# First three batch tiles run group by group, first loads in one line, W turns spread, x turned first

## Chip, cores, metric

One core of one Trainium2 chip. The metric is the device time of one execution in microseconds (us). Ratios are the mean time of one kernel's fast runs over that of the other's fast runs of the same rounds, so they are not quite the ratio of the medians that are quoted beside them.

## The reference

For 4096 rows of 32 vectors of 64 numbers, every pair i < j (496 pairs) has its own 64 x 64 matrix:

```python
idx_i, idx_j = np.triu_indices(F, k=1)          # F = 32, 496 pairs
vi, vj = inputs[:, idx_i, :], inputs[:, idx_j, :]
vidots = jnp.einsum('bpd,pde->bpe', vi, W)
return vidots * vj                              # (4096, 496, 64) float32
```

The output is 520 MB, the inputs 33.6 MB and 8.1 MB.

## The kernel before

A *tile* is 128 batch rows; there are 32, two to an x *block*. Each tile goes through 46 *steps*; a step multiplies x_i with the matrices of up to 16 pairs on PE into PSUM, and then multiplies the result with x_j into an output buffer, on VectorE (DVE), or for some steps by a copy on ScalarE (ACT) and a product on GpSimd (POOL). Five *groups* of steps fill five output buffers' worth, each sent out by one DMA.

W (496 rows of 64 x 64) is loaded in four pieces. Each piece is used only after four *orders* (an SBUF-to-SBUF copy that reorders it) and four *turns* (eight transposes on PE and a copy out of PSUM). x is turned likewise.

```python
groups = [(0, 3), (3, 7), (7, 11), (11, 17), (17, F - 1)]   # 90, 106, 90, 105, 105 pairs
aside = (1, 3, 5, 7, 9, 11, 13)                              # ACT + POOL instead of DVE
xpool = tile_pool(bufs=2); tpool = tile_pool(bufs=3); opool = tile_pool(bufs=3)
...
def load_w(c):
    pool, tag = ((opool, "ot"), (xpool, "xs"), (const, "w3"), (xpool, "xs"))[c]
    ...
    nc.sync.dma_start(out=raw[c][: b - a, :], in_=wflat[a:b])
...
for c, at in enumerate([None, (2, 4, 5, 7), (9, 11, 13, 15), (20, 22, 25, 28)]):
    ...                                   # order and turn k of piece c before step at[k]
new_x(0)
load_x(0, nc.scalar, 0, 1)
load_w(0); load_w(1); load_x(0, nc.sync, 1, NB); load_w(2)
...
for s in range(NBLK * NB * NS):           # tile by tile
    ...
            else:
                c, k = args
                turn_w(c, k, order_w(c, k, (v, p)[k % 2]), a)   # v: DVE, p: POOL, a: ACT
                if k == NU - 1 and c == 1: load_w(3)
                if k == NU - 1 and c == 3: new_x(1); load_x(1, nc.scalar)
    ...
    if pa + m == end:
        nc.sync.dma_start(out=..., in_=ot[:, : end - base, :])
```

Here W pieces 1 and 3 borrow the second x buffer, so x block 1 is loaded last.

## Time and profile before

| | us |
|---|---|
| median of 4 runs | 1359.68 (1359.32 to 1359.97) |
| span of the profiled run | 1357.5 |
| DMA busy from 60 to 1330 us | 99 to 100% |
| bytes | 562.92 MB |

The lines that carry this are in the prediction. Read them with one rule: where DMA is always busy, a microsecond of DMA idle anywhere is a microsecond at the end. In the lines, PEld is PE's weight load, SP is SyncE; SPq and ACTq lines are DMAs being issued on the queue of SP or ACT; `raw` is a loaded piece of W, `rp` an ordered one, `ptw` and `ptx` are turns of W and x in PSUM, `ps` holds products, `ot` is an output buffer, `xs` an x block. Two stretches of the kernel before that the prediction doesn't show, for the comparison below (stretch, its length, busy us of PE, PEld, DVE, ACT and POOL with counts, PE clock, DMA share, GB/s):

```profile
80.00:90.00 10.00, 10.00 (x66) 5.87 (x66) 7.81 (x10) 5.06 (x5) 7.64 (x4) 1.00 1.01 433
90.00:100.00 10.00, 9.20 (x64) 5.57 (x62) 7.19 (x10) 3.04 (x3) 4.78 (x3) 1.00 1.00 428
```

### The profile page before, as it was taken

The page shows a single profiled execution, that of the slowest core. Times are in us where ns is not written, and L with a number is a line of the kernel's source. Part 1 is how long each engine was busy: PE and PEld are TensorE (multiplying, and loading weights), DVE is VectorE, ACT ScalarE, POOL GpSimd, SP SyncE. Part 2 cuts the span into 40 slices and gives each one's busy share as a digit, 9 for nine tenths or more (in the row PEclk, how much of TensorE's full clock was granted, in tenths as well). Part 3 has the DMA queues.
Part 4 walks back from the last instruction along what each step waited for, and adds up shares of the span by engine and source line. Part 5 has one row for each costly group of instructions (what it writes and reads, how often), then busy time and mean ns, then how long its engine had stood idle before and what let it go on. Part 6 is the DMA issues. An engine that isn't in the chain of part 4 may idle for free.

```text
span 1357.5 us, 17867 instructions
## 1 busy us (share of the span) xinstructions
PE 1171.5 (86%) x7424; PEld 681.2 (50%) x7424; DVE 951.3 (70%) x1259; ACT 371.1 (27%) x367; POOL 546.2 (40%) x253
## 2 busy tenths in 40 slices
PE   5998988888888888988889888899888889888894
PEld 4554554545455454554545445455454545545552
DVE  5686876767677676766667767677776777767783
ACT  3432322222222222222322222222222322223220
POOL 4544433443333443334434334433344433444441
PEclk9998998989999999998989999999898999999997
DMA  7999999999999999999999999999999999999997
GB/s 291 388 430 431 426 424 431 431 422 426 401 424 413 430 423 412 428 409 431 410 417 425 413 433 407 421 423 410 428 412 424 426 409 424 406 431 428 417 419 335
DMA packets 26128, 562.92 MB, mean 415 GB/s; under 512 B 2896, under 2 KB 2896, under 8 KB 2896
## 3 DMA queue, kind: packets, MB, share of 16 engines
q1 hardware_dynamic: 23744, 529.28, 92.0%
q10 hardware_dynamic: 2304, 32.51, 5.7%
q8 instruction: 58, 0.95, 0.3%
q14 instruction: 22, 0.18, 0.0%
HBM read 41.68 MB, written 520.09 MB: 414 GB/s over the span
## 4 chain that ended last, share of the span: by engine, by line
DMA 50%; PE 23%; DVE 18%; POOL 4%; issue 3%; ACT 0%; DVEq 0%; SPq 0%; POOLq 0%; ACTq 0%
DMA out_dram<-ot 49%; PE ps L192 19%; DVE ot L209 18%; PE ptx L113 4%; POOL ot L207 3%; DMA raw<-in_L_rec_W_dram 1%; POOL rp L94 1%; PE ptw L103 0%; ACT tmp L206 0%; DVE rp L94 0%; DVEq L209 0%; DVE xT L117 0%; ACT wT L106 0%; SPq L211 0%; POOLq L207 0%
## 5 line engine op out<-in xcount | busy, mean ns | idle before, releaser
L209 DVE TENSOR_TENSOR ot<-ps,xs 128x1024 f32<-128x1024 f32 (+15 forms) x1248 | 938.6, 807 | 378.4 <-DMA out_dram<-ot 195.3
L192 PE MATMUL ps<-wT,xT 64*128 64x512 f32 (+14 forms) x6272 | 1025.2, 467 | 118.0 <-DVE ot L209 105.5
L192 PEld LDWEIGHTS ps<-wT,xT 64*128 64x128 f32 x6272 | 554.0, 193 | 554.6 <-DVE ot L209 281.9
L207 POOL TENSOR_TENSOR ot<-tmp,xs 128x1024 f32<-128x1024 f32 x224 | 527.3, 2360 | 623.5 <-ACT tmp L206 397.7
L206 ACT COPY tmp<-ps 128x1024 f32<-128x1024 f32 x224 | 226.7, 1012 | 465.5 <-PE ps L192 460.6
L117 ACT COPY xT<-ptx 128x1024 f32<-128x1024 f32 x127 | 128.5, 1012 | 470.2 <-PE ptx L113 470.2
L113 PE MATMUL ptx<-ident,xs 128*128 128x128 f32 x1024 | 143.8, 285 | 48.9 <-DVE ot L209 34.3
L113 PEld LDWEIGHTS ptx<-ident,xs 128*128 128x128 f32 x1024 | 113.2, 144 | 95.4 <-issue 51.3
L71 POOL MEMSET xs<- 128x64 f32 x16 | 2.4, 151 | 146.7 <-DVE ot L209 146.7
L94 POOL COPY rp<-raw 128x1024 f32<-128x1024 f32 (+1 forms) x7 | 16.1, 2299 | 16.1 <-DMA raw<-in_L_rec_W_dram 11.8
L106 ACT COPY wT<-ptw 128x1024 f32<-128x1024 f32 (+1 forms) x15 | 14.7, 984 | 28.1 <-PE ptw L103 28.1
L103 PE MATMUL ptw<-ident,rp 128*128 128x128 f32 (+1 forms) x128 | 17.0, 280 | 3.2 <-DVE rp L94 2.0
L94 DVE COPY rp<-raw 128x1024 f32<-128x1024 f32 (+1 forms) x9 | 11.0, 1233 | 12.3 <-DMA raw<-in_L_rec_W_dram 11.9
L103 PEld LDWEIGHTS ptw<-ident,rp 128*128 128x128 f32 (+1 forms) x128 | 14.1, 145 | 10.2 <-issue 5.6
L106 ACT ACT_TABLE_LOAD x1 | 1.3, 1283 | 1.2 <-PEq L229 1.2
L117 DVE COPY xT<-ptx 128x1024 f32<-128x1024 f32 x1 | 1.2, 1208 | 0.0
L106 DVE COPY wT<-ptw 128x1024 f32<-128x1024 f32 x1 | 1.2, 1208 | 0.0
masks.py:197 POOL MEMSET ident<- 128x128 f32 x1 | 0.2, 205 | 0.3 <-POOLq L229 0.3
masks.py:199 POOL TENSOR_SCALAR_AFFINE_SELECT ident<-ident 128x128 f32<-128x128 f32 x1 | 0.3, 292 | 0.0
L229 POOL MEMSET const-float32-0.0<- 128x1 f32 x1 | 0.1, 98 | 0.2 <-issue 0.2
L229 POOL MEMSET const-bfloat16-1.0<- 128x1 bf16 x1 | 0.1, 101 | 0.0
L229 POOL MEMSET const-uint8-127<- 128x1 uint8 x1 | 0.1, 101 | 0.0
(1 smaller groups left out, 0.1 us busy)
## 6 DMA issues: line engine op xcount, KB each, us to landing
out_dram<-ot SPq DMA_DIRECT2D x64, 3360.0 KB, 16.2
out_dram<-ot SPq DMA_DIRECT2D x64, 2880.0 KB, 16.7
out_dram<-ot SPq DMA_DIRECT2D x32, 3392.0 KB, 17.2
xs<-in_r_inputs_dram ACTq DMA_DIRECT2D x15, 2048.0 KB, 16.6
raw<-in_L_rec_W_dram SPq DMA_DIRECT2D x3, 2048.0 KB, 15.6
raw<-in_L_rec_W_dram SPq DMA_DIRECT2D x1, 1792.0 KB, 15.7
xs<-in_r_inputs_dram ACTq DMA_DIRECT2D x1, 1024.0 KB, 11.4
xs<-in_r_inputs_dram SPq DMA_DIRECT2D x1, 1024.0 KB, 17.7
```

Of the source, the lines that this page charges most:

```text
L71: nc.gpsimd.memset(xs[blk][:, 0, :], 0.0)
L94: copy(rp[:r], src[:, k * EU : (k + 1) * EU])
L103: nc.tensor.transpose(pt[:, n, :r], rp[:r, n].rearrange("p h d -> p (h d)"), ident[:r, :r])
L106: copy(wT[c][:, :, k * EU : (k + 1) * EU], pt[:, :, :r].rearrange("p e r -> p r e"))
L113: nc.tensor.transpose(pt[:, n, :], xs[blk][:, s : s + 2, :].rearrange("p f d -> p (f d)"), ident)
L117: copy(xT, pt)
L192: nc.tensor.matmul(ps[:, h, lo - pa : hi - pa, :], xT[blk, kt, n // RUN][h * D : (h + 1) * D, n % RUN, :], wT[c][h * D : (h + 1) * D, lo - ...
L206: nc.scalar.copy(tmp, src)
L207: nc.gpsimd.tensor_mul(dst, tmp, xj)
L209: nc.vector.tensor_mul(dst, src, xj)
L229: nc = _bacc.Bacc("TRN2", target_bir_lowering=False, num_devices=1)
```

## The change

Intent: fill the DMA gap at the start. x is loaded and turned first; all first loads stand in one queue, x block 1 among them; the first three tiles run group by group, so that a piece of W serves three tiles before the next is needed; the first output is cut so that 61 pairs leave early. Because x block 1 now sits in the second x buffer from the start, W piece 3 gets the buffer of piece 2 and is loaded when piece 2 has been ordered.

```diff
-    groups = [(0, 3), (3, 7), (7, 11), (11, 17), (17, F - 1)]
+    bounds = [0, p0[3], p0[6] + CH, p0[11], p0[17], NP]      # 90, 97, 99, 105, 105 pairs
-    tpool = ... bufs=3
+    tpool = ... bufs=4
-        pool, tag = ((opool, "ot"), (xpool, "xs"), (const, "w3"), (xpool, "xs"))[c]
+        pool, tag = ((opool, "ot"), (opool, "ot"), (const, "w3"), (const, "w3"))[c]
+    LEAD = 3
+    sched = [
+        (t, s) for g in range(len(groups)) for t in range(LEAD) for s in range(NS) if steps[s][0] == g
+    ]
+    sched += [(t, s) for t in range(LEAD, NT) for s in range(NS)]
+    for c, orders, turns in (
+        (1, (2, 4, 8, 10), (4, 7, 12, 15)),
+        (2, (17, 22, 27, 32), (19, 24, 29, 34)),
+        (3, (43, 44, 45, 46), (48, 50, 52, 54)),
+    ):
+    no_aside = range(41, 55)
 ...
-    load_x(0, nc.scalar, 0, 1)
+    load_x(0, nc.sync, 0, 1)
     load_w(0)
     load_w(1)
     load_x(0, nc.sync, 1, NB)
     load_w(2)
+    new_x(1)
+    load_x(1, nc.sync)
 ...
+    xT[0, 0, 0] = turn_x(0, 0, 0, a)
+    for k, copy in enumerate((v, v, v, a)):
+        rps[0, k] = order_w(0, k, copy)
+    for k, copy in ((0, a), (3, a), (1, v), (2, a)):
+        turn_w(0, k, rps.pop((0, k)), copy)
 ...
+                rps[c, k] = order_w(c, k, p if c > 1 and k % 2 else v)
+                if (c, k) == (2, NU - 1):
+                    load_w(3, nc.scalar)
 ...
-        if i in aside and c0 == 0:
+        if i in aside and c0 == 0 and s not in no_aside:
+        ends = (p0[2], end) if s < NS and (t, g) == (0, 0) else (end,)
+        if pa + m in ends:                    # first output: 61 and 29 pairs
```

More of the change, by code (lines that the diff above doesn't have):

```diff
@@ L42 @@
     p0 = [i * (F - 1) - i * (i - 1) // 2 for i in range(F)]
-    groups = [(0, 3), (3, 7), (7, 11), (11, 17), (17, F - 1)]
-    cap = max(p0[b] - p0[a] for a, b in groups)
+    bounds = [0, p0[3], p0[6] + CH, p0[11], p0[17], NP]
+    groups = list(zip(bounds[:-1], bounds[1:]))
+    cap = max(b - a for a, b in groups)
     aside = (1, 3, 5, 7, 9, 11, 13)
@@ L55 @@
     xtpool = ctx.enter_context(tc.tile_pool(name="xtpool", bufs=4))
-    tpool = ctx.enter_context(tc.tile_pool(name="tpool", bufs=3))
+    tpool = ctx.enter_context(tc.tile_pool(name="tpool", bufs=4))
     opool = ctx.enter_context(tc.tile_pool(name="opool", bufs=3))
@@ L81, with load_w @@
     NU = E2 // EU
-    def load_w(c: int):
+    def load_w(c: int, eng=nc.sync):
         a, b = wrows[c]
-        pool, tag = ((opool, "ot"), (xpool, "xs"), (const, "w3"), (xpool, "xs"))[c]
+        pool, tag = ((opool, "ot"), (opool, "ot"), (const, "w3"), (const, "w3"))[c]
         raw[c] = pool.tile([P, D * D], F32, tag=tag, name=f"raw_{c}")
-        nc.sync.dma_start(out=raw[c][: b - a, :], in_=wflat[a:b])
+        eng.dma_start(out=raw[c][: b - a, :], in_=wflat[a:b])
     def order_w(c: int, k: int, copy):
@@ L122 @@
         (g, i, c0, min(CH, F - 1 - i - c0))
+        for i in range(F - 1)
+        for c0 in range(0, F - 1 - i, CH)
         for g, (a, b) in enumerate(groups)
-        for i in range(a, b)
-        for c0 in range(0, F - 1 - i, CH)
+        if a <= p0[i] + c0 < b
     ]
@@ L130 @@
         first.setdefault(i, s)
+    LEAD = 3
+    NT = NBLK * NB
+    sched = [
+        (t, s) for g in range(len(groups)) for t in range(LEAD) for s in range(NS) if steps[s][0] == g
+    ]
+    sched += [(t, s) for t in range(LEAD, NT) for s in range(NS)]
+    place = {ts: n for n, ts in enumerate(sched)}
     AHEAD = 4
     due: dict = {}
-    for t in range(NBLK * NB):
+    for t in range(NT):
         for q in range(F // RUN):
-            at = t * NS + (first[q * RUN - 1] if q else 0) - AHEAD
+            at = place[t, first[q * RUN - 1] if q else 0] - AHEAD
             due.setdefault(max(0, at), []).append(("x", t // NB, t % NB, q))
-    for c, at in enumerate([None, (2, 4, 5, 7), (9, 11, 13, 15), (20, 22, 25, 28)]):
-        for k in range(NU) if c else ():
-            due.setdefault(at[k], []).append(("w", c, k))
+    for c, orders, turns in (
[3 rows of a table added]
+    ):
+        for k in range(NU):
+            due.setdefault(orders[k], []).append(("order", c, k))
+            due.setdefault(turns[k], []).append(("turn", c, k))
+    no_aside = range(41, 55)
     LATE = 6
+    loads = {place[blk * NB, LATE]: blk + 1 for blk in range(2, NBLK - 1)}
+    loads[place[LEAD, LATE]] = 2
     new_x(0)
-    load_x(0, nc.scalar, 0, 1)
+    load_x(0, nc.sync, 0, 1)
     load_w(0)
@@ L149 @@
     load_w(2)
+    new_x(1)
+    load_x(1, nc.sync)
     v, p, a = nc.vector.tensor_copy, nc.gpsimd.tensor_copy, nc.scalar.copy
-    xT = {(0, 0, 0): turn_x(0, 0, 0, v)}
+    xT, rps = {}, {}
+    xT[0, 0, 0] = turn_x(0, 0, 0, a)
     due[0] = [d for d in due[0] if d != ("x", 0, 0, 0)]
-    rps = [order_w(0, k, copy) for k, copy in ((0, v), (1, p))]
-    turn_w(0, 0, rps[0], a)
-    rps.append(order_w(0, 2, v))
-    turn_w(0, 1, rps[1], a)
-    rps.append(order_w(0, 3, v))
-    turn_w(0, 2, rps[2], v)
-    turn_w(0, 3, rps[3], a)
-    ot = None
-    for s in range(NBLK * NB * NS):
-        t, st = divmod(s, NS)
+    for k, copy in enumerate((v, v, v, a)):
+        rps[0, k] = order_w(0, k, copy)
+    for k, copy in ((0, a), (3, a), (1, v), (2, a)):
+        turn_w(0, k, rps.pop((0, k)), copy)
+    ots = {}
+    for s, (t, st) in enumerate(sched):
         blk, kt = divmod(t, NB)
         g, i, c0, m = steps[st]
-        if st == LATE and kt == 0 and blk and blk + 1 < NBLK:
-            new_x(blk + 1)
-            load_x(blk + 1, nc.scalar)
+        if s in loads:
+            new_x(loads[s])
+            load_x(loads[s], nc.scalar)
         for what, *args in due.get(s, ()):
@@ L172 @@
                 xT[tuple(args)] = turn_x(*args, a)
+            elif what == "turn":
+                turn_w(*args, rps.pop(tuple(args)), a)
             else:
                 c, k = args
-                turn_w(c, k, order_w(c, k, (v, p)[k % 2]), a)
-                if k == NU - 1 and c == 1:
-                    load_w(3)
-                if k == NU - 1 and c == 3:
-                    new_x(1)
-                    load_x(1, nc.scalar)
-        base, end = p0[groups[g][0]], p0[groups[g][1]]
+                rps[c, k] = order_w(c, k, p if c > 1 and k % 2 else v)
+                if (c, k) == (2, NU - 1):
+                    load_w(3, nc.scalar)
+        base, end = groups[g]
         pa = p0[i] + c0
         if pa == base:
-            ot = opool.tile([P, cap, D], F32, tag="ot", name=f"ot_{t}_{g}")
+            ots[t] = opool.tile([P, cap, D], F32, tag="ot", name=f"ot_{t}_{g}")
+        ot = ots[t]
         ps = psum.tile([P, 2, CH, E2], F32, tag="ps", name=f"ps_{s}")
@@ L209 @@
             nc.vector.tensor_mul(dst, src, xj)
-        if pa + m == end:
+        ends = (p0[2], end) if s < NS and (t, g) == (0, 0) else (end,)
+        if pa + m in ends:
+            n0 = p0[2] if len(ends) > 1 and pa + m == end else base
             nc.sync.dma_start(
-                out=rows_of(out, blk).rearrange("(p k) n d -> p k n d", k=NB)[:, kt, base:end, :],
-                in_=ot[:, : end - base, :],
+                out=rows_of(out, blk).rearrange("(p k) n d -> p k n d", k=NB)[:, kt, n0 : pa + m, :],
+                in_=ot[:, n0 - base : pa + m - base, :],
             )
```

## The prediction

> **What bounds the kernel now.** I read the page's slices first, then ten-microsecond windows of the start, then the order of time.
>
> ```profile
> DMA  7999999999999999999999999999999999999997
> GB/s 291 388 430 431 426 424 431 431 422 426 401 424 413 430 423 412 428 409 431 410 417 425 413 433 407 421 423 410 428 412 424 426 409 424 406 431 428 417 419 335
> HBM read 41.68 MB, written 520.09 MB: 414 GB/s over the span
> ```
>
> Each slice is 34 us. After the first, the DMA engines are busy nine tenths or more and move 400 to 431 GB/s. 562.92 MB at 427 GB/s alone would take 1318 us of 1357.5. So the kernel is bound by the writing of its output, and compute only has to keep that fed. Only the first two slices fall clearly short. The end is no worse: the last output is issued at 1342.1 with about one earlier output still queued.
>
> The windows of the start (columns: stretch, its length, busy us of PE, PEld, DVE, ACT and POOL with counts, PE clock, DMA share, GB/s):
>
> ```profile
> 0.00:10.00 10.00, 0.00 (x0) 0.00 (x0) 0.00 (x0) 1.28 (x1) 0.79 (x7) 1.00 0.85 322
> 10.00:20.00 10.00, 6.10 (x40) 5.66 (x40) 7.91 (x6) 2.94 (x3) 3.83 (x2) 1.00 0.99 424
> 20.00:30.00 10.00, 9.97 (x56) 5.34 (x57) 6.71 (x7) 4.29 (x5) 5.92 (x3) 1.00 0.22 95
> 30.00:40.00 10.00, 10.00 (x69) 6.30 (x69) 6.64 (x7) 5.75 (x7) 6.79 (x4) 1.00 0.97 365
> 40.00:50.00 10.00, 8.34 (x60) 5.37 (x61) 5.46 (x8) 4.93 (x5) 7.87 (x4) 1.00 1.00 363
> 50.00:60.00 10.00, 9.09 (x66) 5.57 (x64) 4.99 (x8) 5.75 (x6) 8.13 (x5) 1.00 1.01 414
> ```
>
> By 60 us 19.83 MB have moved, 46.4 us of work at 427: 13.6 us are lost. 2.5 of these belong to the first ten (nothing moves at once; the change keeps that). **About 11 us can be won at most**: 7.8 in 20 to 30, where the first loads are over and no output is ready, and 3 in 30 to 50, where the last piece of W is read at about 290 GB/s between two outputs. From 60 to 160 us I find no loss.
>
> In that gap PE is the busy engine. In order of time:
>
> ```profile
> 20.03 1.94 PE L192 MATMUL ps<-wT,xT 64*128 64x512 f32 x8 [1.10 <-ACT wT L106]
> ...
> 21.90 1.09 PE L103 MATMUL ptw<-ident,rp 128*128 128x128 f32 x8
> ...
> 22.92 1.88 PE L192 MATMUL ps<-wT,xT 64*128 64x512 f32 x8
> ...
> 29.97 0.35 SPq L211 DMA_DIRECT2D out_dram<-ot  x1
> 30.41 0.38 SPq L88 DMA_DIRECT2D raw<-in_L_rec_W_dram  x1
> ```
>
> From the starts: 31 pairs take 1.87 us (0.0605 us a pair), a turn of eight blocks 1.02 us. Check: the first group is 90 pairs with three W turns, 5.45 + 3.06 = 8.5, so PE should end at 28.5; it ended near 28.6. The second (106 pairs, five turns) should end at 40.1; near 40.4. The output is issued 1.1 to 1.4 us after PE's end. I use this chain below. One pair is 32.8 KB of output, 0.0767 us of DMA, so PE alone outruns DMA; with turns between, it does not.
>
> **What the Trainium skill says.** "DMA: Bandwidth & Descriptors", Specifications, gives a fabric ceiling of 435 GB/s and about 358 GB/s of HBM per core. The trace sides with the first: 431 in whole slices. The same page, Anatomy of one DMA, gives a fixed cost near 2 us, mostly completion. The loads agree: 3.1 MB would be moved near 10 us, and the first W piece is used at 11.93. The same page, Queues, rings and completion order, says that an engine takes turns between queue rows, by packet. The trace agrees: an x load of 2 MB on the second queue takes 16.6 us to land (median) beside outputs. "TensorE: Matmul & The Clock Gate", Part 1, says that PE falls to half clock after an idle window of some 3.4 us. The first eight turns here took 1.94 us, later ones 1.09, though the granted clock reads 1.00; so I allow for it.
>
> **The change part by part.**
>
> *Loads.* All in one line: 1 + 2 + 2 + 1 + 2 + 2 MB = 10.5 MB, moving until 2.5 + 24.6 = 27 us instead of about 22. This brings 5 us of useful traffic forward into the gap; bytes do not change.
>
> *x first.* It lands by about 7, is turned before W arrives at 11.9, and takes one turn and a DVE copy of 1.2 us off the way. Three DVE orders and one ACT order at about 1.0 us, four turns (the first perhaps cold at 1.9) and the last ACT copy of 1.0: the first product at about 19.0 instead of 20.03.
>
> *First output earlier.* It has 61 pairs and waits for the ACT/POOL step (1.0 + 2.4 us). With one x turn ahead of it: PE at 19.0 + 1.87 + 1.02 + 0.97 = 22.9, output at about 26.5. **The gap closes**: loads end at 27.0. It and its 29-pair rest occupy DMA until 33.9.
>
> *Group by group.* Three tiles pass one group of W before the next is needed, so W's sixteen turns spread over three tiles. PE still has to produce (pairs x 0.0605 + turns x 1.02), DMA takes (pairs x 0.0767):
> - Group 0, tiles 1 and 2: 5.45 + 2.04 each; ready 35.3 and 42.8. DMA would be free at 33.9 and 42.3: 1.4 + 0.5 us idle.
> - Group 1 (97 pairs, 5.9 us): two, one and two turns; ready 50.8, 57.7, 65.6. DMA is free at 49.9, then 58.4, 65.8: 0.9 idle.
> - Group 2 needs the last W piece. It shares its buffer with the third and is only issued when that has been ordered, behind the ACT copy of step 29: about 56. At the x loads' 16.6 us, scaled to seven eighths, it lands near 70.7. The order of instructions puts both DVE orders right after step 39, where DVE arrives at about 66.5: **DVE stalls some 4 us**, and PE when its four PSUM buffers are full. Then two orders (2.1) and seven products (6.0): ready near 79 against a DMA free at 78.3, 0.7 idle. Tile 1 must then catch up 3.0 + 1.0 + 6.0 + 3.9 + 1.0 us of PE from about 73.5: ready 89.7 against 86.9, 2.8 idle.
> - Groups 3: 7.4 us of PE for 8.05 of DMA; no idle, slack 1 to 2 us.
> - Groups 4: fourteen small products, all on DVE. Reading their durations (1.22 us for 16 pairs, 0.69 for 8, 0.22 for 1) as 0.066 a pair + 0.17: 6.9 + 2.4 = 9.3 us each for 8.05 of DMA, three in a row: 3.7 us lost less the slack, about 1.7.
>
> Sum: 1.4 + 0.5 + 0.9 + 0.7 + 2.8 + 1.7 = 8.0 us of new waits, plus perhaps 0.5 for the read of W among writes. Of the 11.2 lost before, **some 2.7 us remain as gain**.
>
> *Fourth temporary buffer, groups of 90, 97, 99, 105, 105 instead of 90, 106, 90, 105, 105.* No bytes or products change; 29 tiles run as before, with 41 us of DMA each against 36.6 of PE. I count zero; more even groups may save a little of the last per cent of DMA idle, seen as dips to 385 to 400 GB/s near each x load.
>
> So 1359.6 - 2.7 = 1357; that sum takes every late wait at its worst, so I say **1356**.
>
> **The rivals.**
> - *The gap simply closes* and W lands in time (an emptier queue carries it faster). Then about 3 + 0.5 + 0.5 us are lost, and the gain is about 7: 1352. For it: reads alone ran at 424 GB/s and better. Against it: two outputs are queued when it is issued.
> - *The wait moves*: DMA starves in groups 1, 2 and 4 because the products of the first three tiles hang on PE and W. Gain nought to 2: 1358 to 1360. For it: PE has no margin at all between 19 and 65 us in the sum above. A cold clock after the stall would add 1 to 2 us.
> - *The steady part changes* with the group sizes and the fourth buffer, by up to 5 us either way: 1351 to 1361. For it: the dips exist. Against it: products and bytes per tile are the same, and DVE waited 195 us for outputs to land, so compute mostly has room.
>
> **Range and chances.** The ceiling of the gain is 11 us, 0.8%, so 2% (27 us) is out of reach without a change of the steady part that nothing shows. Slower by 2% would need a stall in every tile. I take 1350 (gap closed, W in time, steady part a bit better) to 1361 (all given back). Faster 0.01, same 0.98, slower 0.01.
>
> **What would show it.** Right: GB/s of 20 to 30 us rises from 95 to above 300; first output issued at 26 to 27 instead of 29.97; first product near 19; a DVE order waiting on the last W load near 66 to 71; DMA dips near 34, 80, 88 and 140; slices from the fifth on as before. Wrong: the W load landing before DVE asks for it (gain nearer 7), or slices past 200 us that differ from before by more than 2 GB/s in the mean (then the steady part has moved, which I do not count on), or a gap in DMA longer than 4 us anywhere.

## The result

| | before | after |
|---|---|---|
| median of 4 runs, us | 1359.68 | 1362.60 (1362.15 to 1362.78) |
| ratio | | 1.0021 (1.0004 to 1.0038) |
| span of the profiled run | 1357.5 | 1360.9 |

Within 2%, but slower, and outside the predicted range. The page's slices of the kernel after:

```profile
DMA  9979999999999999999999999999999999999997
GB/s 380 371 320 432 420 428 433 430 426 426 420 415 423 429 416 414 422 416 424 425 412 417 420 415 426 416 419 412 427 410 421 426 413 424 409 431 421 419 419 318
```

The first slice rose from 291 to 380: the gap at the start is mostly filled. The third fell from 430 to 320: a new hole at 68 to 102 us. The windows of the kernel after (columns as above) place it:

```profile
20.00:30.00 10.00, 10.00 (x56) 5.13 (x54) 8.51 (x8) 3.77 (x4) 2.40 (x1) 1.00 0.87 370
...
50.00:60.00 10.00, 10.00 (x67) 5.90 (x64) 7.96 (x9) 5.07 (x5) 8.88 (x5) 1.00 0.95 368
60.00:70.00 10.00, 7.58 (x50) 4.63 (x48) 4.39 (x5) 3.04 (x3) 2.98 (x2) 1.00 1.00 374
70.00:80.00 10.00, 0.94 (x5) 0.94 (x6) 7.57 (x4) 0.00 (x0) 7.48 (x3) 0.62 1.01 432
80.00:90.00 10.00, 10.00 (x63) 6.54 (x63) 7.99 (x11) 3.53 (x4) 0.24 (x1) 0.87 0.49 207
90.00:100.00 10.00, 10.00 (x80) 6.90 (x78) 8.05 (x11) 4.05 (x5) 3.09 (x2) 1.00 0.67 284
```

PE does nothing from 67.6 to 79 us. DMA lives on what is queued until 80, then is idle half of ten microseconds and a third of the next. In bytes (sum of windows): at 60 us the kernel after is 2.8 MB ahead of before, 6.6 us of DMA; at 100 us it is 1.2 MB behind, 2.9 us. That is the result: **6.6 us won, 9.5 lost again**. The end is 3.4 us later.

What stopped PE, in order of time, kernel after (start us, us, engine, line, operation, in brackets the idle time before and what ended it):

```profile
56.01 0.39 ACTq L89 DMA_DIRECT2D raw<-in_L_rec_W_dram  x1
...
72.43 5.98 DVE L95 COPY rp<-raw 112x1024 f32<-112x1024 f32 x2 [6.81 <-DMA raw<-in_L_rec_W_dram]
72.46 2.77 POOL L95 COPY rp<-raw 112x1024 f32<-112x1024 f32 x1 [6.67 <-DMA raw<-in_L_rec_W_dram]
75.19 2.34 POOL L226 TENSOR_TENSOR ot<-tmp,xs 128x1024 f32<-128x1024 f32 x1
77.59 2.65 POOL L95 COPY rp<-raw 112x1024 f32<-112x1024 f32 x1
78.33 3.47 DVE L228 TENSOR_TENSOR ot<-ps,xs 128x512 f32<-128x512 f32 x4
79.06 1.97 PE L114 MATMUL ptx<-ident,xs 128*128 128x128 f32 x8 [11.48 <-DVE ot L228]
```

The last piece of W is asked for at 56.01 and lands at 72.4. DVE waits for it from 65.6 (6.81 us). Then come two orders on DVE, of which the second takes five times its usual 1.03 to 1.05 us. The chain of waits has it alone:

```profile
73.37 5.04 DVE rp L95
```

In these 5.04 us POOL runs an order and a product, back to back; the DVE order ends 0.9 us after the product. Only then does DVE free a PSUM buffer, and PE, stopped for 11.48 us, goes on at half clock until about 82.6.

**Theory:** the DVE order stands in the instruction line before the W load can have landed; DVE's wait, the two engines' collision after it, and the cold PE make two DMA gaps (from the packet records of the trace: 79.9 to 85.0 and 92.7 to 95.6, together 8.0 us; times of DMA gaps here and below count from a start about 0.8 us after that of the views, so add 0.8 to compare). **Rival 1:** PE has no margin in the first three tiles anyway; taking the wait away only moves the hole. **Rival 2:** the new groups and the fourth buffer slow every tile.

### The profile page after: what moved, and what is told of

Read it like the earlier page. It is cut to its first block, busy times and chain, and to the rows that moved or that the text cites. A ratio compares the mean times of both kernels' runs of the same rounds, so it can differ in the third digit from the quotient of the medians.

```text
span 1360.9 us, 17864 instructions
## 1 busy us (share of the span) xinstructions
PE 1178.6 (87%) x7424; PEld 690.8 (51%) x7424; DVE 960.9 (71%) x1263; ACT 371.5 (27%) x366; POOL 534.4 (39%) x247
## 4 chain that ended last, share of the span: by engine, by line
DMA 49%; PE 27%; DVE 17%; POOL 2%; issue 2%; ACT 0%; DVEq 0%; SPq 0%; POOLq 0%; ACTq 0%
DMA out_dram<-ot 47%; PE ps L211 22%; DVE ot L228 17%; PE ptx L114 4%; POOL ot L226 2%; DMA raw<-in_L_rec_W_dram 2%; PE ptw L104 1%; DVE rp L95 0%; ACT tmp L225 0%; POOL rp L95 0%; DVEq L228 0%; ACT wT L107 0%; SPq L76 0%; SPq L233 0%; POOLq L226 0%
## 5 line engine op out<-in xcount | busy, mean ns | idle before, releaser
L211 PE MATMUL ps<-wT,xT 64*128 64x512 f32 (+13 forms) x6272 | 1033.7, 473 | 131.6 <-DVE ot L228 120.3
L211 PEld LDWEIGHTS ps<-wT,xT 64*128 64x128 f32 x6272 | 563.8, 197 | 566.6 <-DVE ot L228 305.3
L225 ACT COPY tmp<-ps 128x1024 f32<-128x1024 f32 x221 | 223.9, 1013 | 505.6 <-PE ps L211 462.2
L95 DVE COPY rp<-raw 128x1024 f32<-128x1024 f32 (+1 forms) x11 | 15.1, 1410 | 18.1 <-DMA raw<-in_L_rec_W_dram 18.1
L95 POOL COPY rp<-raw 128x1024 f32<-128x1024 f32 (+1 forms) x4 | 9.4, 2350 | 6.7 <-DMA raw<-in_L_rec_W_dram 6.7
## 6 DMA issues: line engine op xcount, KB each, us to landing
xs<-in_r_inputs_dram ACTq DMA_DIRECT2D x14, 2048.0 KB, 16.6
```

What stands on the lines that cost most here:

```text
L95: copy(rp[:r], src[:, k * EU : (k + 1) * EU])
L211: nc.tensor.matmul(ps[:, h, lo - pa : hi - pa, :], xT[blk, kt, n // RUN][h * D : (h + 1) * D, n % RUN, :], wT[c][h * D : (h + 1) * D, lo - ...
L225: nc.scalar.copy(tmp, src)
```

## The experiments

Eleven kernels, all with the right result. They ran on three chips, four, four and three to a chip, beside the kernel before, whose median there was 1360.32, 1359.65 and 1359.99. The kernel after was not run again beside them; the kernel before stood at 1359.68 beside it, so differences from 1362.60 below can be off by some 0.6 us.

One thing was not expected: **the kernel before has two groups of times**. Of its 33 runs in these calls, six stood at 1364.2 to 1365.3 and the others at 1359.1 to 1361.2, all in the fast state. The means hold both, so the ratios below flatter the experiments by up to 0.1%; medians are the better guide.

### e1: the orders of the last piece later

```diff
-        (3, (43, 44, 45, 46), (48, 50, 52, 54)),
+        (3, (57, 58, 59, 60), (61, 63, 65, 67)),
-    no_aside = range(41, 55)
+    no_aside = range(55, 68)
```

> The last W piece's orders are moved from steps 43-46 to 57-60, its turns from 48-54 to 61-67 (it is first needed at step 75); nothing else. Theory (DVE stands in front of a W load that lands at 72.3, and what follows starves DMA from 80 to 85 and 93 to 96): DVE comes to the order after the load has landed, no DVE order waits over 1 us on that load, DMA is busy from 62 to 110 us without a gap over 1 us, and the time falls by about the two gaps, 4.75 + 2.95 us: 1362.6 to about 1354.5 (1353 to 1356.5). Rival (PE has no margin in the first three tiles, so any order of the W work starves DMA by as much, only elsewhere): gaps of about 8 us in sum come later, between 85 and 160, and the time stays at 1360 to 1363.

Measured: **1354.37 us** (1354.22 to 1354.91), ratio 0.9948 (0.9932 to 0.9963), against an expected 1354.5. The deferred kernel's windows, over the same stretch:

```profile
80.00:90.00 10.00, 9.23 (x62) 5.54 (x62) 10.00 (x10) 2.15 (x3) 4.87 (x2) 0.94 1.03 443
90.00:100.00 10.00, 10.00 (x74) 6.06 (x72) 7.03 (x10) 4.51 (x5) 0.97 (x1) 1.00 0.96 410
```

207 and 284 GB/s have become 443 and 410. No hole came later: the packet records show less than 0.05 us of idle from 110 to 165. Rival 1 falls. The later placing of the four orders and four turns is worth 8.2 us, nearly three times the loss. (The stretch in which DVE takes all products, `no_aside`, moved along with them; its share was not tested alone.)

### e2: the load on the SP queue, ahead of an output

```diff
-                    load_w(3, nc.scalar)
+                    load_w(3, nc.sync)
-        (2, (17, 22, 27, 32), (19, 24, 29, 34)),
+        (2, (17, 22, 27, 30), (19, 24, 29, 34)),
```

> The last W load goes to the SP queue, ahead of the second output of group 1 (its buffer's last order moved from step 32 to 30), so it doesn't share the engines packet by packet with outputs. Orders and turns stay at 43-54. Theory: issued near 56 it starts when the output before it is done (about 58.5) and lands at 65 to 68 instead of 72.3; DVE waits 0 to 2 us instead of 6.8; the gaps at 80 and 93 shrink to 0 to 2 us in sum; time about 1356 (1354.5 to 1358). Rival (the wait is not the cause, PE's margin is): DVE no longer waits but the time stays at 1360 or above. Rival (the load is slow whatever its queue, for it reads 112 rows): it lands at 70 or later and the time stays within 1 us of 1362.6.

Measured: **1358.06 us** (1357.37 to 1358.94), ratio 0.9975. Orders after the landing, in this kernel's order of time:

```profile
67.52 5.96 DVE L95 COPY rp<-raw 112x1024 f32<-112x1024 f32 x2 [2.38 <-DMA raw<-in_L_rec_W_dram]
67.57 2.72 POOL L95 COPY rp<-raw 112x1024 f32<-112x1024 f32 x1 [2.27 <-DMA raw<-in_L_rec_W_dram]
...
74.13 1.97 PE L114 MATMUL ptx<-ident,xs 128*128 128x128 f32 x8 [7.03 <-DVE ot L228]
```

The piece lands 4.9 us earlier (67.5), DVE waits 2.38 instead of 6.81, and all that follows is earlier by as much. The time fell by 4.5 us, two short of expected, because the 5.96 us of orders stayed: PE still stood 7.03 us. So the late landing, which DVE waits for, is about one half of the cause. The reason of that lateness, the sharing of the DMA engines between two queues, is supported too: 16.3 us to land beside outputs, 12 in line with them.

### e3: the four orders all on DVE

```diff
-                rps[c, k] = order_w(c, k, p if c > 1 and k % 2 else v)
+                rps[c, k] = order_w(c, k, p if c == 2 and k % 2 else v)
```

> All four orders of the last W piece on DVE, none on POOL. The load lands as late as before (72). Theory, second part (the second DVE order took 5.04 us instead of 1.05 because POOL's copy and product held the way they share): every DVE order takes 1.0 to 1.1 us, the first product after the stall comes at about 75 instead of 78.4, PE begins again at about 75.5 instead of 79.1, and the time falls by 2 to 4 us, to about 1359.5. If the 5 us were instead the tail of the load (data still landing), the order stays long and the time within 0.7 us of 1362.6.

Measured: **1360.95 us** (1360.71 to 1361.66), 1.65 below the kernel after, a little less than expected (2.3 if the chips' 0.6 us is counted). In this kernel's order of time:

```profile
72.38 1.96 DVE L95 COPY rp<-raw 112x1024 f32<-112x1024 f32 x2 [6.77 <-DMA raw<-in_L_rec_W_dram]
74.26 0.68 DVE L228 TENSOR_TENSOR ot<-ps,xs 128x512 f32<-128x512 f32 x1
74.86 1.98 DVE L95 COPY rp<-raw 112x1024 f32<-112x1024 f32 x2
75.00 1.97 PE L114 MATMUL ptx<-ident,xs 128*128 128x128 f32 x8 [7.42 <-DVE ot L228]
```

With the same landing, each order takes 1.02 to 1.04 us, and PE begins at 75.0 instead of 79.1. The long order was not the tail of the load; it was POOL. Only 1.65 of these 4 us reached the end: the DMA gaps become 2.5 and 3.95 us. That PE is still cold and DVE has two orders more is the likely reason, not tested.

### e4: the new groups and the fourth buffer alone

The kernel before, with the new `bounds`, the loop over steps that they need, and `bufs=4`.

> The kernel before with only the new group bounds (90, 97, 99, 105, 105) and the fourth temporary buffer. Theory (the steady part of the kernel is not touched by the change; all of the +3 us come from the first three tiles): 1359.7 within 0.8 us. Rival (the new groups or buffer slow or quicken every tile): 1357 or less, or 1361.5 or more, with a rate over 180 to 1330 us that differs by over 0.2% from before.

Measured: five runs at 1365.55 to 1366.21, **one at 1360.72**. The time fits the rival, but not the rate from 180 to 1330 us: 420.3 GB/s against 419.9 before, a difference of 0.1%. Neither held as written, until the two traces were laid side by side near 47 us, where tile 0 orders the last piece of W. The kernel before (profiled at 1359.5):

```profile
46.18 1.03 DVE L94 COPY rp<-raw 112x1024 f32<-112x1024 f32 x1
46.23 2.81 POOL L94 COPY rp<-raw 112x1024 f32<-112x1024 f32 x1 [1.20 <-DMA raw<-in_L_rec_W_dram]
```

and this one (profiled at 1366.2):

```profile
46.98 1.89 POOL L95 COPY rp<-raw 112x1024 f32<-112x1024 f32 x1 [1.13 <-PE ps L194]
47.04 5.02 DVE L95 COPY rp<-raw 112x1024 f32<-112x1024 f32 x1
48.84 2.34 POOL L209 TENSOR_TENSOR ot<-tmp,xs 128x1024 f32<-128x1024 f32 x1
```

Where DVE is 0.05 us ahead, its order takes 1.03 us and POOL's 2.81. Where POOL is 0.06 us ahead, DVE waits through POOL's order and the product behind it: 5.02 us. A race of a twentieth of a microsecond decides 5 us, and a DMA gap of 5.2 us follows in the second trace (52.4 to 57.6).

### e8 and e9: the same race taken out of the kernels without grouping

e8 is the kernel before, e9 is e4, each with:

```diff
-                turn_w(c, k, order_w(c, k, (v, p)[k % 2]), a)
+                turn_w(c, k, order_w(c, k, (v, p)[k % 2] if c < 3 else v), a)
```

> The kernel before with only the last W piece's orders all on DVE. The kernel before has two groups of times on this chip, 7 of 11 runs at 1359.6 to 1360.8 and 4 at 1364.3 to 1365.3. In the profile of the run with the new groups alone (1366 us) the first DVE order of the last piece took 5.02 us, begun 0.06 us after POOL's; in the profile of before (1359.5) it took 1.03, begun 0.05 us ahead of POOL's. Theory (a race between the two for the shared way decides the 5 us): with no POOL order there, all runs are within 1.2 us of each other at 1359 to 1361, none above 1362. If a group at 1364 to 1366 remains, the two groups have another cause.

(The counts in it are wrong: three of those 11 runs were at 1364 to 1365, eight at 1359.6 to 1360.8.) Measured: **1359.70 us**, five runs within 0.5 us. The upper group didn't come; with six of 33 in the kernel before, five runs alone would not prove it.

> The kernel with the new groups and the fourth buffer alone, now with the last W piece's orders all on DVE. Theory (its 1366 us were the lost race between DVE and POOL near 47 us, not the groups): all runs at 1359.2 to 1361, no group at 1365. Rival (the groups cost 5 us): the times stay at 1365 to 1366.

Measured: **1361.99 us** (1361.82 to 1362.42). Where e4 had five of six at 1366, this has none. So the race made e4's upper group, and by likeness perhaps the one of the kernel before, of which no slow run has a profile. But the expectation missed: 1362.0 is 2.0 above the kernel before beside it. Are the new groups (or the fourth buffer) the cost? e4's one fast run speaks against it: 1360.72, only 0.4 above the kernel before. The 2 us may come only with the orders on DVE; no run separates this. It is not a cost of every tile: of the 2.1 us in span against e8, 1.3 are there at 60 MB and 1.4 at 562 of 563 MB, the rest is in the last rows. Rival 2 may be right in this small part.

### e10: the changed start alone

e9, with x first on the SP queue, the four orders and turns of W piece 0 as in the change, and the first output cut in 61 and 29 pairs; tile by tile.

> The previous kernel plus the changed start alone: x0 first on the SP queue, turned by ACT, four W orders on DVE and ACT, and the first output cut in 61 and 29 pairs; tile by tile, x1 late, as before. The start part alone moves the first output forward by 2 to 3 us: DMA's gap runs from 22.6 to about 27.3 instead of 30; its time comes to 1357 (1356.3 to 1358.8). If grouping or the early x block were needed for that gain, it stays at 1359.5 or above.

Measured: **1361.02 us** (1360.77 to 1362.21). Missed: the first output did come at 26.0 and DMA's gap there shrank from 7.45 us to 4.4 against e9, but a gap of 2.8 us stands at 48 to 50.9 where e9 has 0.75. Won 3.05, lost 2.05; the medians differ by 1.0. In tile-by-tile order all sixteen W turns still stand in tile 0, and from the issue of its group 1 output to that of group 2 it takes 12.1 us in both kernels (38.72 to 50.84, in e9 40.22 to 52.31), so the earlier start meets an empty DMA queue. That the grouping is what turns an early start into time is an inference: e1 has both, but it also loads x block 1 early, and no run has the grouping alone.

### e5, e6, e7: from the deferred kernel on

e5 is e1 with the orders as in e3. e6 is e1 with PE kept at work while W piece 0 loads:

```diff
+    warm = psum.tile([P, RUN, P], F32, tag="ps", name="warm")
+    for n in range(20):
+        nc.tensor.transpose(warm[:, n % RUN, :], ident, ident)
```

e7 has both.

> The deferred kernel (1354.4 us) with the last W piece's four orders all on DVE. In the deferred kernel's trace the two DVE orders still took 5.41 us beside POOL's, but DMA had work queued and stood idle only 1 us between 80 and 110. Theory (what counts is DMA idle, and the long order is POOL's hold on the shared way): each order takes 1.0 to 1.1 us or waits at most one POOL product of 2.4; idle between 80 and 110 falls below 0.5 us; the time falls by at most 1 us, to 1353.4 to 1354.4. If the time falls by over 2 us, DMA idle isn't the whole account.

Measured: **1354.30 us** (1353.95 to 1356.31), as good as e1, and each order took 1.04 to 1.06 us, both as expected: an order's length counts only where DMA runs dry. Missed: the idle from 80 to 110 us did not fall below 0.5 us (0.96, in e1 0.98).

> The deferred kernel with twenty turns of the identity, whose results nobody reads, put on PE between the first x turn and the first W turn, so that PE isn't idle there. Why the first product came at 19.80 and not at the predicted 19.0: the 32 W turns took 6.30 us where four warm ones take 4.1. Theory (PE runs at half speed there after its idle time): the 32 turns take 4.2 to 5.0 us, the first product comes at 18.4 to 18.9, the first output a microsecond earlier, and the idle stretch near 34 to 36 shrinks; time lower by 0.5 to 1.2 us, 1353.2 to 1353.9. If the 32 turns still take 6 us, they hang on the orders of DVE and ACT and the time stays.

Measured: 1354.02, 1354.10, 1357.34, 1359.26, 1359.53, 1359.90. The 32 turns of W piece 0, first in the kernel after, then in e6:

```profile
12.40 6.30 PE L104 MATMUL ptw<-ident,rp 128*128 128x128 f32 x32 [3.92 <-DVE rp L95]
```

```profile
12.00 3.78 PE L104 MATMUL ptw<-ident,rp 128*128 128x128 f32 x32 [0.70 <-DVE rp L95]
```

The half clock is shown. In the kernel after, the first 24 of these transposes start 0.213 us apart and the last eight 0.108; in e6 all 32 start 0.11 apart. The first product comes at 16.9 instead of 19.8 (19.2 in e1). Yet the time spread upward. In the profiled run (1359.5) the two DVE orders of the last piece took 7.21 us beside POOL's: in e1 (5.41 us) POOL stood idle for 0.59 us between its order and its product, and DVE's copy got through in 2.29; here the product followed at once, and the copy took 4.55. But this is not all: 1.4 us more DMA idle than in e1 stand before 60 us, ahead of these orders, and why is not shown.

> Both of these together with the deferral, as the best version: 1352.5 to 1353.7 us, 0.995 of before or less, and no two groups of times.

Measured: **1354.34 us**, five runs at 1354.15 to 1354.47 and one at 1358.04, without a profile. A miss on both counts: not 1352.5 to 1353.7, and one run apart. Without POOL's orders most of the upper times are gone, but nothing was won by the warm start. PE had met the next wait, the landing of x block 1 (this kernel's order of time):

```profile
29.20 1.06 PE L114 MATMUL ptx<-ident,xs 128*128 128x128 f32 x8 [1.81 <-DMA xs<-in_r_inputs_dram]
```

### e11: and the first turn of x block 1 three steps later

```diff
-            at = place[t, first[q * RUN - 1] if q else 0] - AHEAD
+            at = place[t, first[q * RUN - 1] if q else 0] - (1 if (t, q) == (2, 0) else AHEAD)
```

> The version with deferral, DVE orders and warm PE (1354.3), and the turn of the second x block's first eight moved three steps later, for PE stood 1.8 us before the landing of that block at 29.1. Theory: PE goes on without that wait, the second tile's first output is issued 1.5 to 2.5 us earlier and the DMA gap at 33.7 to 35.4 shrinks below 0.5 us; time about 1352.8 (1352.2 to 1353.6). If the idle comes back elsewhere before 110 us, the time stays within 0.5 us of 1354.3.

Measured: **1352.33 us** (1352.07 to 1352.54, six runs), ratio 0.9940 (0.9928 to 0.9952): the best kernel here, and its runs show no second group. Its windows:

```profile
20.00:30.00 10.00, 10.00 (x56) 5.12 (x53) 9.21 (x10) 4.74 (x5) 3.25 (x2) 1.00 1.00 420
30.00:40.00 10.00, 10.00 (x58) 5.35 (x57) 8.42 (x9) 4.35 (x5) 5.14 (x3) 1.00 1.02 437
```

DMA is busy from the first loads on; the gap of the kernel before (22.75 to 30) is gone, and none over 1 us has taken its place.

### The ledger of all kernels

From the packet records of each profiled run: the time in which an engine of the 16 had no packet, averaged over the 16, from the start to 165 us; and the span.

| kernel | idle to 165 us | span | span less idle |
|---|---|---|---|
| before | 9.7 | 1357.5 | 1347.8 |
| after | 13.5 | 1360.9 | 1347.4 |
| e1 deferred | 5.5 | 1352.7 | 1347.2 |
| e2 SP queue | 7.8 | 1356.3 | 1348.5 |
| e3 DVE orders | 12.2 | 1359.6 | 1347.4 |
| e4 groups alone | 16.0 | 1364.4 | 1348.4 |
| e5 | 5.5 | 1352.5 | 1347.0 |
| e6 | 10.7 | 1357.7 | 1347.0 |
| e7 | 5.6 | 1352.5 | 1346.9 |
| e8 before, DVE orders | 10.1 | 1357.9 | 1347.8 |
| e9 groups, DVE orders | 10.7 | 1360.0 | 1349.3 |
| e10 start alone | 9.2 | 1359.0 | 1349.8 |
| e11 best | 3.5 | 1350.4 | 1346.9 |

The idle time runs from 3.5 to 16.0 us, and what is left varies by 3. Nearly all that these thirteen kernels differ in is DMA idle time in the first 110 us. The two that stand 1.5 to 2 us above the kernel before, e9 and e10, have the new groups without the grouping; e4 has them too and stands only 0.6 above.

## Why the prediction was wrong

It was wrong in sign: a gain of 2.7 us by its sum was a loss of 2.9.

- **What bounds the kernel** was right: e1 to e11 follow DMA's idle time. Microseconds of engine work (the orders in e5, PE's clock in e7) moved nothing where DMA had work queued.
- **Start.** First product 19.0 predicted, 19.80 measured; three of the four turns were at half clock, not one (6.30 us, not about 5). First output 26.5 predicted, 27.46 measured; DMA idle there 0.9 us instead of none.
- **Groups 0 and 1.** Idle of 1.4 + 0.5 + 0.9 us predicted; the records show one gap of 1.7 (34.65 to 36.35) and 0.8 in scraps. PE's chain held.
- **The last W load.** Issue at 56 predicted, 56.01 measured; landing at 70.7, 72.4 measured; DVE there at 66.5, 65.6 measured. The wait was seen, and its cause; it took 6.8 us, not some 4.
- **The step that failed** is the next one: "Then two orders (2.1) and seven products (6.0): ready near 79 against a DMA free at 78.3, 0.7 idle." The two orders took 5.98 us, PE came back at half clock, and the output was ready at 85.0: 5.05 us idle. The 2.1 was two times the duration of an order that runs alone. (The DMA free at 78.3 can't be worked out from the text: 65.8 + 7.44 for the last output of group 1 + 4.3 for the 1.84 MB of W gives 77.5; DMA ran dry at 80.8 on the same clock.) The kernel before had an order of 2.81 us beside a POOL order, at 12 us, the second of these two; I took it for none of my concern:

```profile
11.93 3.77 DVE L94 COPY rp<-raw 128x1024 f32<-128x1024 f32 x2 [11.93 <-DMA raw<-in_L_rec_W_dram]
11.96 2.82 POOL L94 COPY rp<-raw 128x1024 f32<-128x1024 f32 x1 [10.62 <-DMA raw<-in_L_rec_W_dram]
```

The Trainium skill has the rule on a page that I had not opened ("SBUF — State Buffer", Who interferes with whom): DVE copies can take a pair of ports that POOL uses too; whoever starts first holds it, and the other "fully blocks". e3 agrees (1.02 to 1.04 us each without POOL's orders).
- **Catching up in tile 1**, 2.8 us predicted, 2.95 measured. Right, with its time later by six.
- **Group 4**, 1.7 us predicted, none seen (less than 0.05 us of idle from 110 to 165). DVE's fourteen products are slower than DMA, but enough was queued.
- **The read of W among writes**: "perhaps 0.5 us". The windows from 50 to 70 us ran at 368 and 374 GB/s; against 427 this is 2.6 us (with most of the 0.8 in scraps above). The deferred kernel pays it too (359 and 383).
- **The steady part**: net nothing, as predicted, though not so plainly. At 60 MB written the kernel after is 3.2 us behind, at 562 MB 1.5, at the end 3.4: it gains 1.7 on the way and loses 1.9 in the last rows. The kernels with the new groups all take 8.7 to 9.6 us from 562 MB to the end, those with the old 7.4 to 8.1. Why, no run tells.

Summed: the failed step is worth 4.35 us and the read of W 2.1; the others take off 1.5 (0.9 - 1.1 + 0.15 - 1.7 + 0.2). That is 4.9 of the 6.1 us between the gain of 2.7 and the loss of 3.4 in span; 1.2 stay unaccounted for. Two more slips of the prediction, without weight: its slices after the first run from 388 to 433 GB/s and end with 335, not 400 to 431; and 56 + 7/8 of 16.6 is 70.5, not 70.7.

Of the rivals, the second ("the wait moves") came nearest (1362.6 lies above even its 1358 to 1360), but in group 2 alone and for another reason than it gave: PE's lack of margin was not to blame (e1); the cold clock it named was there, and its share was not tested. The first is what the change does once the orders stand later: 1354.4, where I had said 1352.

Left open: whether the kernel before's upper times are the lost race (shown only in e4 against e9), and to what the 2 us of e9 belong.

## What to carry to other kernels

An in-order engine that is given an instruction whose data is still on the way stops everything behind it; when a change moves a load later, move its first reader too, and count from the landing time measured beside other traffic. Durations are only worth what ran beside them: a copy that takes 1.03 us alone took 5 beside another engine, and a race for it can split a kernel's times in two groups. When the bound is DMA, write the ledger of its idle time; a gain of 6.6 us at 60 us and a loss of 9.5 at 100 look like "the same" from outside.

## What the Trainium skill lacked or had wrong

- "SBUF — State Buffer", Who interferes with whom, says that the loser waits until the other has finished. Here DVE waited through *two* POOL instructions on end (5.02 and 5.04 us: an order of 1.9 to 2.8 and a product of 2.34). POOL took the ports again before the waiting DVE copy got them; I found no page that warns of that. It got them where POOL paused: for 0.59 us in e1, or after a single product (3.2 us in e7, e8, e9 and e11).
- The same section says that issue order decides. Agreed, with its price: 0.05 us ahead, 1.03 us; 0.06 us behind, 5.02 us, and 5 us of the kernel's time.
- "TensorE: Matmul & The Clock Gate", Part 1: right in its substance (the 32 transposes took 6.30 us after idling, 3.78 when PE was kept busy; after the stop at 67.6 us the clock read 0.50 until 82.6, 3.5 us after PE went on). The granted clock in the profile read 1.00 in the cold stretch at 12 to 18 us, so that column alone would have hidden it: the trace's first clock record comes only at 17.75 us, where the transposes quicken.
- "DMA: Bandwidth & Descriptors", Specifications: the 358 GB/s of HBM per core (half of what two cores share) is no limit for one core that runs alone; whole slices ran at 431 to 433.
- I found no page with what a load costs in the middle of outputs: 1.8 MB took 16.3 us to land on the second queue, 12 on the queue of the outputs (e2), and 15.7 there in the kernel before, issued 0.4 us after an output. "DMA: Bandwidth & Descriptors" tells how queues take turns, but gives no such time.
